# A two-layer graph network: layer 1's factor blocks loaded in two pieces instead of four

## The chip, the cores and the metric

The kernel runs on one core of a Trainium2 chip. The metric is the time of one execution on the device, in microseconds (us). The engines that matter here: TensorE (PE in the profile; its weight loads are PEld) multiplies matrices into eight accumulator banks, VectorE (DVE), ScalarE (ACT) and GpSimd (POOL) work elementwise, and SyncE (SP) issues nearly all transfers between the device's memory and the on-chip memory. Each engine works through its own queue in order; between engines, instructions wait on semaphores.

## The reference

128 samples, each with 128 nodes of 512 features (`x`, 128 x 128 x 512) and a 128 x 128 adjacency (`adj`). Two layers, all in float32:

```python
# layer 0
deg = sum(adj, -1)
agg = (adj @ x) / max(deg, 1e-6)
x = layernorm(x + relu(concat([x, agg], 2) @ W.T))       # W is 512 x 1024
# layer 1
Xw = x @ Wv + bv
e = leaky_relu(sj[:, None, :] + si[:, :, None] + ab[0])   # sj, si = Xw @ halves of aw
t = adj * exp(e);  t = t / (sum(t, -1) + 1e-12)
H = x @ Wk[0] + bk[0] + (t @ x) @ Wk[1] + bk[1] + (t @ t @ x) @ Wk[2] + bk[2]
x = layernorm(x + relu(H))
```

## The kernel before

**Groups and layers.** Four samples make a group, so each layer has 32 groups, numbered 0 to 31 in layer 0 and 32 to 63 in layer 1. Layer 0 runs for all groups, its results go to device memory (`yd`), and layer 1 reads them back.

**The products.** Each large product is done by a fast scheme for 2 x 2 blocks, applied twice: seven outer products (called 1 to 7), each made of seven inner products (k = 1 to 7). An outer product is a task that yields after each inner one: in layer 0 `P12`, `P56`, `P74` do two outer products each, and `T` (function `last`) does product 3 and the multiplication by the normalised adjacency; in layer 1 `O1` to `O7` do one each, and `C` combines. Tables `LEFT` and `RIGHT` say which of the seven sums of a factor the inner product k reads: RIGHT gives 0, 4, 5, 2, 1, 3, 6 in the order in which k is run (1, 5, 6, 2, 7, 3, 4).

**Where the right factors lie.** One tile, `big`, holds them. In layer 0 it is seven slots of 7 x 256 columns (`wf`, table `SLOT`). In layer 1 each outer product o has a block of 7 x 385 columns, `wg[o]`, at the column that `AT` gives. Blocks 1, 2 and 5 lie where the raw weights of layer 1 were staged and which is free long before; blocks 6, 7, 4 and 3 lie one after the other from column 0 on, over the slots of layer 0. So these four can only be loaded as layer 0's last group gives its slots up: slots 0 and 1 are read by `P12`, 2 and 3 by `P56`, 4 and 5 by `P74`, 6 by `T`. The blocks are made earlier, by GpSimd beside layer 0, and are kept in device memory (`wds`, the profile's `wd`). `wg_load(o, i)` brings piece i of block o back. `outer` (L618) asks that all four pieces of its block are issued.

**The order of the work.** It is written out by hand. `PA`, `PT`, `PG`, `PB`, `PL` list the steps of TensorE for a group of layer 0, for the last group of layer 0 with the first of layer 1, and for the groups of layer 1. All else (loads, stores, sums) is placed at a position, two positions to a step, by tables `PLACES_...`. `PLACES_T` (L1038) places the pieces: block 1 at -467, -448, -408 and -388, block 2 at -351, -316, -304 and -263, block 5 at -200, -173, -148 and -104, block 6 at -32, -31, -4 and -2, block 7 at 26, 23, 20 and 65, block 4 at 31, 54, 73 and 46, block 3 at 53, 79, 88 and 85 (pieces 0, 1, 2, 3 each), counted from the start of `PT`. The position decides the order within SyncE's queue, not the time: SyncE runs ahead until an instruction has to wait.

**Around it in SyncE's queue.** `y_store` (L571, issue on L576) stores a half group's result of layer 0 once ScalarE has normalised it (`ln_apply`, L517). `load_y` (L91, issue on L95) loads the input rows of the next half group into one of two buffers, so it waits for the store from that buffer. `residual` (L378, VectorE, L380) adds the product to that y and frees the accumulator bank that the product was in. `load_left` (L86, issue on L83) loads the left factor, `a_load` (L609, also L83) the turned adjacency.

**The steps of one product of layer 1** (`outer`): the first inner product goes to bank X, and ScalarE copies X to bank Y (L628); the second goes to Z and is copied or, with the bias, added by VectorE to `s5` (L632, L634); the third accumulates in X, and VectorE writes W = X + s5 (L637); and so on. In layer 0 `pair` does the same with lines L314, L317, L320 and L326. The banks of `T`, freed by the residuals of group 31, are those that O5 of group 32 takes.

Of the kernel before, what the change touches and what calls it, by code (L numbers as in the profile page):

```python
# [16 lines left out]
def kernel(  # L17
# [219 lines left out]

    def wg_load(o, i):
        assert len(wds) == 7
        k = slice(2 * i, min(2 * i + 2, 7))  # L240
        nc.sync.dma_start(wg[o][:, k], wds[o][:, k])


# [645 lines left out]
    for g in range(1, NG):  # L889
        base[g] = len(steps)  # L890
        for s in PA:
            name, k = s.split(".")
# [8 lines left out]
    for s in PT:  # L901
        name, k = s.split(".")
# [3 lines left out]
    for g in range(NG):  # L906
        base[NG + g] = base[NG] + len(PB) * g
        for s in PL if g == NG - 1 else PB if g else PG:
            name, k = s.split(".")
# [137 lines left out]
    for (name, o, i), pos in PLACES_T.items():  # L1047
        at(max(2 * start_b + pos, 2 * base[NG - 1]) if NG < 20 else 2 * start_b + pos, wg_load, o, i)
# [52 lines left out]
```

## Time and profile before

| | |
|---|---|
| median of 3 runs | 2068.39 us (2068.28 to 2069.03) |
| profiled execution | 2068.23 us, its span 2066.5 us |
| granted TensorE clock | 0.999 |
| TensorE busy | 2053.8 us, 99% of the span |
| VectorE, ScalarE, GpSimd busy | 1515.5, 1161.4, 1374.6 us |
| moved by DMA | 287.14 MB |
| loads of factor blocks (L241) | 21 of 385 KB, 7 of 192.5 KB, from 622.7 to 818.5 us |

The span is the time from the first to the last instruction. A view's line gives the start and the duration in us, the engine, the line of the kernel, the operation, the tiles (written <- read), the shapes, how many alike follow each other, and in brackets the idle time before and what ended it. A DMA's duration on SyncE's queue is that of its issue; its landing comes later. Layer 0 ends and layer 1 begins at about 802 to 820 us.

### The profile page before, as it was taken

Reading aid. Unit: us, or ns where it says so; the run is one execution under the profiler, and the core shown is the slowest. Engines: PE = TensorE matmul, PEld = TensorE weight load, DVE = VectorE, ACT = ScalarE, POOL = GpSimd, SP = SyncE. Lnnn points to the kernel's source line nnn. Section 1 sums busy time; section 2 is a strip of 40 time slices with the busy share of each in tenths; the row PEclk is TensorE's granted clock in tenths of the full one; section 3 lists DMA queues with packets and bytes.
Section 4 is the critical chain, followed back from the end, with each engine's and each line's share of the span. In section 5 each row is a group of like instructions: output and inputs, shape, how many; then the busy total and the mean of one; then the engine's idle time right before and its main releaser. Section 6 shows DMA issues by size and latency. Waiting matters only on the chain.

```text
span 2066.5 us, 25981 instructions
## 1 busy us (share of the span) xinstructions
PE 2053.8 (99%) x7108; PEld 1338.4 (65%) x7108; DVE 1515.5 (73%) x3418; ACT 1161.4 (56%) x2872; POOL 1374.6 (67%) x1263
## 2 busy tenths in 40 slices
PE   9999999999999999999999999999999999999998
PEld 6878888888887887555555555555555555555554
DVE  6787777787878777667767767767766766766766
ACT  2666666666666666455455455455455455455454
POOL 5877888887777776756656656656656656656652
PEclk9999999999999999999999999999999999999999
DMA  9777766666667777434534534534534534534623
GB/s 202 176 192 189 187 188 176 158 190 190 165 162 197 181 189 228 108 88 112 129 88 109 132 88 112 128 88 112 128 88 113 128 88 113 128 87 112 129 75 110
DMA packets 431071, 287.14 MB, mean 139 GB/s; under 512 B 155593, under 2 KB 353865, under 8 KB 430924
## 3 DMA queue, kind: packets, MB, share of 16 engines
q1 hardware_dynamic: 429996, 284.15, 55.6%
q10 hardware_dynamic: 800, 1.31, 0.3%
q8 instruction: 56, 0.92, 0.2%
q14 instruction: 91, 0.75, 0.1%
q0 software_dynamic: 128, 0.01, 0.0%
HBM read 191.60 MB, written 93.79 MB: 138 GB/s over the span
## 4 chain that ended last, share of the span: by engine, by line
PE 98%; DMA 1%; DVE 1%; issue 0%; POOL 0%; ACT 0%; ACTq 0%; SPq 0%; DVEq 0%
PE bA L155 51%; PE bB L155 47%; DMA xb<-in_x_dram 0%; DMA big<-in_w0t_dram 0%; PE bA L181 0%; DVE big L1024 0%; DVE c L458 0%; PE bA L167 0%; DVE c L366 0%; ACT y L562 0%; POOL rs L539 0%; DVE dg L730 0%; DVE bA L475 0%; DVE y L380 0%; DVE xl L259 0%
## 5 line engine op out<-in xcount | busy, mean ns | idle before, releaser
L155 PE MATMUL bB<-big,xu 128*128 128x385 f32 (+1 forms) x1806 | 556.8, 433 | 0.1
L155 PEld LDWEIGHTS bB<-big,xu 128*128 128x128 f32 x1806 | 342.6, 190 | 159.8 <-issue 24.4
L155 PE MATMUL bA<-big,xl 128*128 128x256 f32 (+1 forms) x1358 | 406.0, 416 | 0.6 <-DVE bA L475 0.6
L155 PE MATMUL bB<-big,xs 128*128 128x256 f32 (+1 forms) x1316 | 389.0, 416 | 0.0
L155 PEld LDWEIGHTS bA<-big,xl 128*128 128x128 f32 x1358 | 256.5, 189 | 100.5 <-issue 15.3
L155 PEld LDWEIGHTS bB<-big,xs 128*128 128x128 f32 x1316 | 249.6, 190 | 84.1 <-issue 1.7
L155 PE MATMUL bA<-big,xu 128*128 128x256 f32 (+1 forms) x896 | 287.0, 432 | 0.1
L155 PE MATMUL bA<-c,TT 128*128 128x512 f32 x512 | 240.7, 592 | 0.0
L504 ACT ACTIVATE junk<-y,mv 128x512 bf16<-128x512 f32 x252 | 181.7, 721 | 88.9 <-POOL mv L499 82.6
L499 POOL TENSOR_SCALAR mv<-mv 128x4 f32<-128x4 f32 x63 | 14.4, 228 | 313.0 <-DVE y L380 313.0
L155 PEld LDWEIGHTS bA<-big,xu 128*128 128x128 f32 x896 | 166.5, 189 | 76.6 <-DVE bA L397 5.0
L517 ACT ACTIVATE y<-y,mv,rstd 128x512 f32<-128x512 f32 x252 | 204.7, 814 | 3.6 <-POOL mv L512 1.7
L637 DVE TENSOR_TENSOR bB<-bB,s 128x385 f32<-128x385 f32 x128 | 72.6, 567 | 170.9 <-ACT s L634 73.4
L380 DVE SCALAR_TENSOR_TENSOR y<-bA,y 128x512 f32<-128x512 f32 x253 | 165.7, 681 | 12.0 <-PE bA L155 7.4
L155 PE MATMUL bB<-big,xl 128*128 128x385 f32 (+1 forms) x462 | 172.1, 480 | 0.4 <-ACT bA L456 0.4
L805 POOL TENSOR_TENSOR T<-ag,T 128x512 f32<-128x512 f32 x31 | 39.5, 1274 | 198.7 <-ACT T L800 145.8
L155 PE MATMUL bA<-big,xs 128*128 128x385 f32 x448 | 167.9, 491 | 0.0
L155 PEld LDWEIGHTS bA<-c,TT 128*128 128x128 f32 x512 | 96.8, 189 | 88.8 <-issue 47.6
L270 POOL TENSOR_TENSOR xs<-xl 128x896 f32<-128x896 f32 x63 | 131.4, 2085 | 21.4 <-PE bB L155 21.4
L849 ACT COPY bA<-r 128x512 f32<-128x512 f32 x62 | 36.5, 589 | 190.7 <-DVE big L847 190.6
L282 POOL TENSOR_TENSOR xu<-xu,xs 128x896 f32<-128x896 f32 x63 | 131.5, 2087 | 9.3 <-PE bB L155 9.3
L278 POOL TENSOR_TENSOR xl<-xu,xl 128x896 f32<-128x896 f32 x63 | 133.4, 2117 | 1.1
(206 smaller groups left out, 3614.2 us busy)
## 6 DMA issues: line engine op xcount, KB each, us to landing
xb<-in_x_dram SPq DMA_DIRECT2D x256, 128.0 KB, 3.8
y<-in_x_dram SPq DMA_DIRECT2D x64, 512.0 KB, 4.3
yd<-y SPq DMA_DIRECT2D x64, 512.0 KB, 3.0
xb<-yd SPq DMA_DIRECT2D x256, 128.0 KB, 6.5
y<-yd SPq DMA_DIRECT2D x64, 512.0 KB, 6.8
out_dram<-y SPq DMA_DIRECT2D x62, 512.0 KB, 3.3
ag<-in_adj_dram SPq DMA_DIRECT2D x63, 256.0 KB, 6.0
sb<-sd SPq DMA_DIRECT2D x252, 64.0 KB, 3.3
```

The lines of the kernel that those rows point to most:

```text
L155: nc.tensor.matmul(dst, lhsT, rhs, start=start, stop=True, skip_group_check=True)
L270: S_.tensor_add(xs[n][:, 0], xl[n][:, 0], xl[n][:, 1])
L278: S_.tensor_sub(xl[n][:, 0], xu[n][:, 0], xl[n][:, 0])
L282: S_.tensor_sub(xu[n][:, 1], xu[n][:, 1], xs[n][:, 1])
L380: V.scalar_tensor_tensor(y, t, 0.0, y, ALU.max, ALU.add, accum_out=mvs[n][:, b, 0:1])
L499: S_.tensor_scalar(mvs[n][:, :, 0], mvs[n][:, :, 0], -1.0 / F, None, ALU.mult)
L504: L_.activation(junk, ys[n, b // 2][:, b % 2], AF.Square, bias=mvs[n][:, b, 0:1], accum_out=mvs[n][:, b, 1:2])
L517: L_.activation(y, y, AF.Identity, bias=mvs[n][:, b, 0:1], scale=rstds[n][:, b : b + 1])
L637: V.tensor_add(W, X, s5)
L805: S_.tensor_mul(T, adjs[NG + g], T)
L849: L_.copy(to[b], row(b, 254, 766, 1))
```

## The change

Of the four calls of `wg_load` for a block, the two with odd i do nothing. The call with i = 0 loads inner factors 0 to 3 (770 KB), the one with i = 2 factors 4 to 6 (577.5 KB). The positions stay, so factors 2 and 3 are loaded at the place of piece 0 and factor 6 at the place of piece 2.

```diff
     def wg_load(o, i):
         assert len(wds) == 7
-        k = slice(2 * i, min(2 * i + 2, 7))
+        if i % 2:
+            return
+        k = slice(2 * i, min(2 * i + 4, 7))
         nc.sync.dma_start(wg[o][:, k], wds[o][:, k])
```

## The prediction

> **What bounds the kernel now.** I read the page first: the busy shares and the chain that ended last.
>
> ```profile
> PE 2053.8 (99%) x7108; PEld 1338.4 (65%) x7108; DVE 1515.5 (73%) x3418; ACT 1161.4 (56%) x2872; POOL 1374.6 (67%) x1263
> ...
> PE 98%; DMA 1%; DVE 1%; issue 0%; POOL 0%; ACT 0%; ACTq 0%; SPq 0%; DVEq 0%
> ```
>
> TensorE is busy all the way and the chain is 98% TensorE. Then the list of waits, for TensorE alone:
>
> ```profile
> PE bA L152 <- POOL ident masks.py:199: 2.7, 1, 2.7
> PE bA L155 <- DVE bA L475: 0.6, 2, 0.3
> PE bB L155 <- ACT bA L456: 0.4, 1, 0.4
> ```
>
> These are all the waits of TensorE that the list has: 3.7 us, all at the very start, and none is for a load of a factor block. So there is hardly anything to win: the change can move the time only by opening a hole in TensorE's row. The question is which transfer comes later, and whether anybody on TensorE's path is waiting for it.
>
> Third, the timeline of SyncE's queue where layer 0 ends and layer 1 begins:
>
> ```profile
> 785.85 0.34 SPq L241 DMA_DIRECT2D big<-wd  x1
> 786.87 0.36 SPq L576 DMA_DIRECT2D yd<-y  x1
> 787.33 0.42 SPq L241 DMA_DIRECT2D big<-wd  x1
> 787.84 3.47 SPq L95 DMA_DIRECT2D y<-in_x_dram  x2
> ...
> 802.55 1.34 SPq L241 DMA_DIRECT2D big<-wd  x3
> 808.13 0.37 SPq L576 DMA_DIRECT2D yd<-y  x1
> 808.60 0.41 SPq L241 DMA_DIRECT2D big<-wd  x1
> 809.54 0.37 SPq L576 DMA_DIRECT2D yd<-y  x1
> 811.30 3.53 SPq L95 DMA_DIRECT2D y<-in_x_dram  x2
> 814.92 4.31 SPq L241 DMA_DIRECT2D big<-wd  x8
> ```
>
> By the positions in PLACES_T, 785.85 and 787.33 are pieces 0 and 1 of block 6; the three at 802.55 are pieces 2, 1, 0 of block 7; 808.60 is piece 0 of block 4; the eight at 814.92 are the rest of blocks 7, 4 and 3. Between them stand stores of y of group 30 (L576) and loads of y of group 31 (L95), which go into the buffers that those stores empty: a load of y cannot be issued before the store has landed.
>
> Last, VectorE, ScalarE and TensorE where that y is used (start, duration, engine, line, operation, tiles, shapes, count, idle time before):
>
> ```profile
> 815.82 0.69 DVE L380 SCALAR_TENSOR_TENSOR y<-bA,y 128x512 f32<-128x512 f32 x1 [0.57 <-PE bA L155]
> ...
> 820.14 0.65 DVE L380 SCALAR_TENSOR_TENSOR y<-bA,y 128x512 f32<-128x512 f32 x1
> ...
> 822.88 0.56 DVE L637 TENSOR_TENSOR bA<-bA,s 128x385 f32<-128x385 f32 x1
> ...
> 820.90 0.46 ACT L628 COPY bA<-bA 128x385 f32<-128x385 f32 x1 [3.86 <-DVE y L380]
> ...
> 821.83 1.46 PE L155 MATMUL bA<-big,xs 128*128 128x385 f32 x4
> ...
> 823.77 0.81 PE L155 MATMUL bA<-big,xs 128*128 128x385 f32 x2
> ```
>
> The load of y issued at 811.30 takes 4.4 us to land (the tile's own view), so it lands at 815.74; the matmul that the residual at 815.82 also needs had ended at 815.54. This residual starts 0.08 after the landing: it is already waiting for y, not for TensorE. From there VectorE runs without a gap until 823.44.
>
> **The change, part by part.** Bytes first: before 21 loads of 385 KB and 7 of 192.5 KB, after 7 of 770 and 7 of 577.5, both 9,432.5 KB. 14 issues go. At a median of 431 ns each that is 6.0 us of SyncE, worth nothing: SyncE is waiting for ScalarE or VectorE both before and after each of these places (after the eight at 814.92 its next instruction is at 828.61, held by ScalarE). If that cover were gone the gain would be at most the 1.0 us of TensorE's other start-up waits, which no such load causes: 0.
>
> *Blocks 1, 2, 5 (622 to 754 us).* They go to memory that was free long before, and are first read at 803.8 or later. Pieces 0 and 1 of block 1 were issued back to back already. Piece 1 of block 2, now at 662.30, stands ahead of the load of y at 662.85 that lands 5.35 later, at 668.20, with its residual at 670.09: 1.9 us in hand against the 0.98 us worked out below. Block 5's stands ahead of four loads (sb) that are used more than ten microseconds later; block 1's last, half as large, ahead of one load of y. Cost 0; at the slower rate below, 2.06, at worst 0.2.
>
> *Block 6.* SyncE's own list of waits shows that these loads wait for layer 0's products:
>
> ```profile
> SPq L241 <- PE bB L155: 3.7, 4, 2.7
> ```
>
> The longest, 2.7 us, ends at 785.85, when the product that reads factor 3 of slot 0 is done. The new piece also covers factor 6, which the next product reads: SyncE waits four matmuls longer, which the chain has at 0.86 us, and the store of y at 786.87 stands behind 770 KB. The loads of y of group 30 (787.84 and 790.94) come 0.4 to 0.9 us later, and so do their residuals at 793.62 and 795.93, which end on a landing of y already. Behind them in VectorE's queue the first operation that TensorE needs soon is L326, 798.80 to 799.50, for a matmul at 800.32. Idle gaps of 0.40 and 0.17 us in the queue swallow part, the 0.8 ahead of the matmul the rest. Cost 0; if the second y came 1.3 late and no gap helped, 0.5.
>
> *Block 7.* Piece 3 comes forward from position 65 to 20: 192.5 KB more at 802.55. The region was last read by P56, whose last matmul ends at 801.35, so no new wait. The first of the three loads lands 3.7 after its issue, at 806.2, the others 0.98 each behind it, 808.2; 0.5 more, or 0.9 with what block 6 hands on, is 809.1. The store issued at 808.13 begins to move at 809 only (the DMA share of 808 to 809 is 0.00). Cost 0, at worst 0.2.
>
> *Block 4, the one that costs.* At 808.60 the load becomes 770 KB. The store of y at 809.54 stands behind it, and behind that the load of y issued at 811.30. For the rate I take the stretch in which nothing but such loads moves (us, busy times by engine, clock, DMA share, GB/s):
>
> ```profile
> 805.00:807.00 2.00, 2.00 (x8) 1.43 (x8) 1.04 (x3) 1.54 (x4) 1.92 (x2) 1.00 1.02 404
> ...
> 810.00:812.00 2.00, 2.00 (x8) 1.08 (x6) 1.03 (x4) 1.20 (x3) 2.00 (x2) 1.00 0.92 191
> ```
>
> 385 KB (394,240 bytes) at 404 GB/s are 0.98 us. From 812 to 815 the DMA engines are fully busy with these transfers in turn, so the lateness goes through: y lands at 816.72 and the residual moves from 815.82 to 816.80. The second row, the stretch in which this very load starts, would give 2.06 us; it is nearest in place, but I read its slow part as the start of a transfer, which a longer one pays once, so I take 0.98 and keep 2.06 as the upper end. Lower end 0, if transfers of one queue do not hold each other up; a gain is excluded, since nothing ahead of this y becomes smaller.
>
> What it does to TensorE: VectorE has no gap, so all behind it moves by 0.98. ScalarE's copy at 820.90, into the bank that the third residual frees, goes to 821.88 to 822.34. The matmul at 821.83 (third product of O5) overwrites the copy's source and must wait. Where the trace shows such a pair, the copy that ends at 805.08 and the matmul after it at 805.23, 0.15 lies between. So 822.49 instead of 821.83: 0.66. Then VectorE's L637 ends at 824.42 instead of 823.44, and the matmul that waits for it, due at 823.77 + 0.66, starts at 824.57: 0.80 in all. VectorE's next idle 1.19 us (before 824.62) ends the chain. With 2.06 the same steps give 825.65 against 823.77: 1.9.
>
> *Blocks 4 and 3, the rest.* After the last load of y come three transfers of 1,925 KB in all instead of eight of 2,502.5 KB; they land earlier than the 825.5 of before. O4's first two products run from 832.2, O3's from 838.6: 7 us in hand. Cost 0.
>
> Sum: the profiled execution took 2068.23 us (span 2066.5 and 1.7 around it), 0.16 under the median of the runs, 2068.39. Adding 0.80 to the median gives **2069.2 us**. Ends: 0, and 1.9 + 0.5 + 0.2 + 0.2 = 2.8.
>
> **Two rules of the Trainium skill.** The eight loads at 814.92 are issued over 3.6 us and the last lands 6.9 us after its issue, at 825.5: their waiting times overlap. "DMA: Bandwidth & Descriptors", section "Anatomy of one DMA", gives each transfer (fitted on GpSimd's path) about 2.0 us of fixed cost besides its bytes; 14 fewer would by that be an estimated 28 us gained if they ran one by one. By the row above they don't, and nobody waits for them: 0. Against the change speaks "Perfetto Trace Analysis", section "DMA Optimizations": pieces may let some work start sooner. That would matter for the blocks' own first products; with 7 us in hand the sum by it is the same 0.
>
> **The rivals.** All within or beyond 0.2%, which is 4.1 us and about what a measurement of this kernel can tell from no change.
> 1. *Hidden after all:* the rings share their time, the y is late by under 0.2 us, no hole. For it: ScalarE's copy ends 0.47 us before the matmul that needs it, so the first 0.3 us of lateness cost nothing. Against: the load of y at 811.30, with two transfers ahead of it, took 4.4 us, the next one, with less ahead, 3.6. Time 2068.4, with 0.3 either way.
> 2. *A larger hole, 1.5 to 4.1 us:* the slow rate of 191 GB/s and the late store of block 6 add up: 1.9 + 0.5. Time about 2070.8. Against: the 0.8 us that the matmul at 800.32 has in hand.
> 3. *Slower by over 0.2%:* the load of y at 811.30 comes so late that VectorE's queue holds TensorE for more than 4.1 us. It decides from a lateness of 4.1 + 0.2 = 4.3 us, that is 394,240 bytes at 92 GB/s. No stretch with such packets is that slow here. Time from 2072.6.
> 4. *Faster by over 0.2%:* would need 4.1 us back, and TensorE waits for 3.7 in all, at the start.
>
> **How the numbers follow.** Chances: forecast (a hole of 0.3 to 1.5) 0.55, rival 1 0.27, rival 2 0.10, rival 3 0.06, rival 4 0.02. Within 0.2% are the first three, 0.92; slower 0.06; faster 0.02. Rival 1's lower edge is 2068.1; the forecast's own range is 2068.7 to 2069.9. The range 2068.0 to 2070.5 takes in both, and the near part of rival 2.
>
> **What the profile after would show.** The 14 loads; the load of block 4 at about 808.6 with a landing near 5.5 us instead of 4.5; the load of y after it landing about 1 us later; the residual of 815.82 near 816.8; a new row of TensorE's waits for ScalarE L628 or VectorE L637, under 1 us, near 822 to 825. If TensorE has no new gap there and the time stays, rival 1 was right. I am wrong if TensorE stands still elsewhere: at 800 (block 6), at 832 or 838 (a block that came too late), or in layer 0.

## The result, and the profile after

| | before | after |
|---|---|---|
| median (range), 19 runs each | 2068.2 us (2067.93 to 2069.03) | 2071.49 us (2070.32 to 2073.3) |
| span of the profiled execution | 2066.5 us | 2069.3 us |

The ratio is 1.0016, with a 95% interval of 1.001 to 1.0023. The kernel lost 3.3 us; 2069.2 was forecast, and the range ended at 2070.5. The loss is less than the 0.2% that the prediction drew as its bound, but it is a loss.

The page of the kernel after, its busy times and the shares of the chain that ended last:

```profile
PE 2053.9 (99%) x7108; PEld 1339.7 (65%) x7108; DVE 1515.3 (73%) x3418; ACT 1160.9 (56%) x2872; POOL 1374.8 (66%) x1263
...
PE 97%; DMA 1%; DVE 1%; issue 0%; ACT 0%; POOL 0%; ACTq 0%; SPq 0%; DVEq 0%
```

No engine works longer: TensorE has 0.1 us more than before. So the 2.8 us of span are time in which TensorE stood still. Its list of waits, after (engine, tile, line, what it waited for: us in total, times, longest):

```profile
PE bA L152 <- POOL ident masks.py:199: 2.7, 1, 2.7
PE bA L155 <- DVE y L382: 1.6, 2, 1.1
PE bA L155 <- DVE big L1018: 0.7, 1, 0.7
PE bA L155 <- ACT bA L630: 0.7, 1, 0.7
PE bA L155 <- DVE bA L477: 0.6, 2, 0.3
PE bB L155 <- ACT bA L458: 0.4, 1, 0.4
```

(Lines of the kernel from L241 on count two more after the change: the residual L380 is now L382, ScalarE's copy L628 is L630, the load of a block L241 is L243.) New are the two waits for the residual, L382, and the one for the copy, L630. The 0.7 for L1018 lies at the start of the program, where the profiles of the other kernels below have 0.3 to 0.5 or nothing; since no matmul up to 791 starts later than before, it has nothing to do with the loss. The timeline of TensorE, after, has the three holes (start, duration, tiles, shapes, count, and in brackets the idle time before and its end):

```profile
795.77 1.13 PE L155 MATMUL bA<-big,xl 128*128 128x256 f32 x4 [0.50 <-DVE y L382]
...
822.52 0.91 PE L155 MATMUL bA<-big,xs 128*128 128x385 f32 x2 [1.08 <-DVE y L382]
823.27 0.81 PE L155 MATMUL bB<-big,xu 128*128 128x385 f32 x2
824.75 1.56 PE L155 MATMUL bA<-big,xs 128*128 128x385 f32 x4 [0.67 <-ACT bA L630]
```

The brackets count from the modelled end of the matmul before. What a hole really costs is read better from the starts of the same matmuls in the two timelines:

| matmul of before | before | after | after minus before |
|---|---|---|---|
| T's multiplication by the adjacency | 791.70 | 791.67 | -0.03 |
| second product of outer 4, layer 0 | 796.01 | 796.74 | 0.73 |
| first product of O5 | 819.90 | 820.63 | 0.73 |
| the product after the hole at 822.52 | 821.19 | 823.27 | 2.08 |
| third product of O5 | 821.83 | 824.75 | 2.92 |
| 3 us later | 825.07 | 828.22 | 3.15 |

So nothing is lost before 791; 0.76 at 795.77, 1.35 at 822.52, 0.84 at 824.75 and 0.2 more behind it: 3.2 us in all. The spans of the two profiled executions differ by 2.8, the medians by 3.3. From 828 to 860 the difference does not grow, so nothing is lost at 832 or 838: no factor block came too late.

What made those residuals late is in SyncE's queue, after:

```profile
786.68 0.34 SPq L243 DMA_DIRECT2D big<-wd  x1
787.12 0.39 SPq L578 DMA_DIRECT2D yd<-y  x1
787.60 5.88 SPq L95 DMA_DIRECT2D y<-in_x_dram  x2
793.57 0.42 SPq L588 DMA_DIRECT2D sd<-an  x1
...
798.32 3.07 SPq L83 DMA_DIRECT2D sb<-sd  x4
801.49 4.58 SPq L83 DMA_DIRECT2D xb<-yd  x4
806.17 0.87 SPq L243 DMA_DIRECT2D big<-wd  x2
808.86 0.37 SPq L578 DMA_DIRECT2D yd<-y  x1
809.33 0.41 SPq L243 DMA_DIRECT2D big<-wd  x1
810.27 0.82 SPq L578 DMA_DIRECT2D yd<-y  x1
814.18 4.02 SPq L95 DMA_DIRECT2D y<-in_x_dram  x2
```

Read beside the rows of before, this gives the chain. (When the store of y at 787 landed is not in the trace; it is taken from the load that waits for it and that is issued right behind.)

| | before | after |
|---|---|---|
| block 6's first load issued | 785.85 | 786.68 |
| the store of y behind it issued, landed | 786.87, 790.92 | 787.12, 793.09 |
| the load of y into the emptied buffer issued | 790.94 | 793.10 |
| residuals of group 30 that wait for y | 793.62 and 795.93 | 795.02 and 797.48 |
| the store sd<-an issued; the loads of sb, which wait for its landing | 792.14; 796.55 | 793.57; 798.32 |
| the first load of xb behind them issued, and how long its issue took | 799.49, 1.49 | 801.49, 3.09 |
| block 7's first load issued | 802.55 | 806.17 |
| the store of y issued, its landing after | 808.13, 3.1 | 808.86, 5.2 |
| the load of y of group 31 issued, landed | 811.30, 815.74 | 814.18, 819.08 |
| the residual of O5's bank | 815.82 | 819.15 |
| ScalarE's copy behind it | 820.90 | 824.24 |

Block 6's load was issued 0.83 later, and was twice as large. The store behind it was issued only 0.25 later but landed 2.17 later, and the next load of y can't be issued until it has landed. While SyncE waited for that, the DMA engines ran out of work. Windows of both kernels, first before (us, then busy times of TensorE, its weight loads, VectorE, ScalarE, GpSimd, then the clock, the DMA share and GB/s):

```profile
786.00:789.00 3.00, 3.00 (x16) 2.60 (x15) 2.56 (x9) 2.22 (x7) 2.38 (x2) 1.00 0.71 212
793.00:796.00 3.00, 3.00 (x10) 1.69 (x9) 1.98 (x6) 0.00 (x0) 0.72 (x1) 1.00 1.01 309
801.00:805.00 4.00, 4.00 (x18) 3.01 (x16) 3.74 (x10) 1.94 (x5) 2.97 (x5) 1.00 0.88 195
```

and after:

```profile
786.00:789.00 3.00, 3.00 (x16) 2.60 (x15) 2.60 (x9) 2.18 (x7) 2.36 (x2) 1.00 0.46 68
793.00:796.00 3.00, 2.50 (x7) 0.94 (x6) 0.98 (x3) 0.00 (x0) 0.72 (x1) 1.00 0.62 196
801.00:805.00 4.00, 4.00 (x20) 3.43 (x19) 3.87 (x10) 2.24 (x6) 3.65 (x7) 1.00 1.02 147
```

Where the engines were full, at a share of 1.01, they are at 0.62. That work was not saved but pushed on, and the lateness grew from 0.83 to 3.62 us: the two landings that SyncE waits for brought 2.0 of it (the loads of sb and xb), and the single issue of 3.09 us at 801.49 the other 1.6. In that stretch the DMA engines were full (1.02). Whether they held the issue up or a wait for VectorE, to which the list of SyncE's waits puts 3.1 us there, is open. Block 7's loads left at 806.17, ahead of the store of y at 808.86, which itself was issued only 0.73 later. The Trainium skill, "DMA: Bandwidth & Descriptors", section "Two DMAs through the same engine are not ordered", says that within one queue of one DMA engine the descriptors start in order. The row of the store at 787.12 agrees: with 770 KB ahead of it, where there were 385, it landed 5.97 us after its issue instead of 4.05.

The timeline of VectorE, after, shows the three late residuals (in brackets, what ended the idle time):

```profile
795.02 0.69 DVE L382 SCALAR_TENSOR_TENSOR y<-bA,y 128x512 f32<-128x512 f32 x1 [2.72 <-DMA y<-in_x_dram]
...
797.48 0.69 DVE L382 SCALAR_TENSOR_TENSOR y<-bA,y 128x512 f32<-128x512 f32 x1 [0.54 <-DMA y<-in_x_dram]
...
819.15 0.69 DVE L382 SCALAR_TENSOR_TENSOR y<-bA,y 128x512 f32<-128x512 f32 x1 [3.17 <-PE bB L155]
```

The first frees at 795.71 the bank that outer 4's first product takes at 795.77. In the kernel before it ended at 794.31 and the product started at 795.15: 0.84 in hand, used up. The third bracket names a product of TensorE, but that is not the releaser: its y landed at 819.08, 0.07 before the residual. The engine named had long been done.

### The profile page after: what moved, and what is told of

Read it like the earlier page. It is cut to its first block, busy times and chain, and to the rows that moved or that the text cites. A ratio compares the mean times of both kernels' runs of the same rounds, so it can differ in the third digit from the quotient of the medians.

```text
span 2069.3 us, 25959 instructions
## 1 busy us (share of the span) xinstructions
PE 2053.9 (99%) x7108; PEld 1339.7 (65%) x7108; DVE 1515.3 (73%) x3418; ACT 1160.9 (56%) x2872; POOL 1374.8 (66%) x1263
## 4 chain that ended last, share of the span: by engine, by line
PE 97%; DMA 1%; DVE 1%; issue 0%; ACT 0%; POOL 0%; ACTq 0%; SPq 0%; DVEq 0%
PE bA L155 50%; PE bB L155 47%; DMA xb<-in_x_dram 0%; DMA y<-in_x_dram 0%; DMA big<-in_w0t_dram 0%; PE bA L181 0%; DVE y L382 0%; ACT junk L599 0%; DVE big L1026 0%; DVE c L460 0%; PE bA L167 0%; DVE c L671 0%; DVE c L368 0%; ACT y L564 0%; POOL rs L541 0%
## 5 line engine op out<-in xcount | busy, mean ns | idle before, releaser
L382 DVE SCALAR_TENSOR_TENSOR y<-bA,y 128x512 f32<-128x512 f32 x253 | 165.7, 681 | 16.0 <-PE bA L155 5.2
```

The costliest lines, as they stand in the source:

```text
L382: V.scalar_tensor_tensor(y, t, 0.0, y, ALU.max, ALU.add, accum_out=mvs[n][:, b, 0:1])
```

## The experiments

**Theories.** A: each enlarged load holds up the store and the load of y behind it in SyncE's queue. It begins at block 6; the delay is handed on through the gate "a load of y is issued when the store has landed" to block 7's and block 4's place, and TensorE stands where the late y's banks are needed. B, the rival: the blocks act one by one, without handing on, and block 6 costs little. A further question was whether it is the bytes or the longer rows (6,160 bytes for each of 128 partitions and load, where there were 3,080), and for block 6, whether the bytes or the wait for one more product.

The kernel before was run beside them and had medians of 2068.2 to 2068.6, so differences below 0.3 us are not read. The ratios' intervals are about 0.1% to either side, 2 us. By them alone only the change, block 6 alone and "block 6 later" have intervals clear of 1. For the others the reading rests on the medians of ten runs together with the holes in the profile. A profile shows one of the ten, and not always a typical one: those of the exchange of pieces below and of block 7 alone are of a short execution, those of blocks 1, 2 and 5 and of all blocks as short loads of a long one. Holes are counted from the starts of the same matmuls, from T's multiplication by the adjacency on (791.70 in the kernel before).

### One part alone

Each is the kernel before, with this in place of the one line, for the blocks in the brackets:

```diff
-        k = slice(2 * i, min(2 * i + 2, 7))
+        if o in (6,):              # (1, 2, 5) / (7,) / (4,) / (1, 2, 5, 7, 4, 3)
+            if i % 2:
+                return
+            k = slice(2 * i, min(2 * i + 4, 7))
+        else:
+            k = slice(2 * i, min(2 * i + 2, 7))
```

**Blocks 1, 2 and 5 alone.**

> Blocks 1, 2 and 5 in two pieces, the other four blocks in four as before. Both theories: nothing waits for these loads and what is queued behind them has slack, so no hole in TensorE's row and the time of before, 2068.2 us (0.2 either way). If over 0.5 us of the 3.3 us show here, a third cause lies in layer 0.

Measured 2068.30 (2068.06 to 2068.96) beside 2068.34: 0.0. By the median the early loads cost nothing and gain nothing. Its profile, of an execution of 2068.92, does have a hole, against the expectation: 0.55 at 796.

```profile
PE bA L155 <- DVE y L385: 0.3, 1, 0.3
```

Nothing near 796 was changed here; the first load of y took 6.9 us to land there instead of 5.7. So a hole of half a us at this place also comes without a larger load, and one such hole in a profile proves little. Those of the change and of block 6 alone are 0.8 to 0.9.

**Block 6 alone.**

> Block 6 alone in two pieces. Theory A (one delay that is handed on): the load waits for one more product, moves twice the bytes ahead of a store of y, and from there all of SyncE's queue runs late: a hole of about 0.8 us at 796, the loads of block 7 issued about 3 us later than 802.55, the residual of 815.82 late by about 2 us and a second hole of 1 us or more at 822; time 2069.8 to 2071.2. Theory B (each block costs by itself, where it stands): only the hole at 796, 0.8 us; time 2069.0.

Measured 2070.29 (2069.57 to 2070.87): +1.95, ratio interval 1.0001 to 1.0019. This is more than half of the whole loss, from a block that the prediction gave 0. Its queue of SyncE:

```profile
786.45 0.34 SPq L246 DMA_DIRECT2D big<-wd  x1
786.88 0.39 SPq L581 DMA_DIRECT2D yd<-y  x1
787.36 5.96 SPq L95 DMA_DIRECT2D y<-in_x_dram  x2
...
806.15 1.34 SPq L246 DMA_DIRECT2D big<-wd  x3
...
813.52 2.60 SPq L95 DMA_DIRECT2D y<-in_x_dram  x2
```

The three loads of block 7 are those of the kernel before, unchanged, and still leave at 806.15 instead of 802.55 (802.3 to 803.4 in all profiles with block 6 in four pieces at its old places); the load of y of group 31 leaves at 813.52 instead of 811.30. TensorE waits at both places, though only the first was touched:

```profile
PE bA L155 <- DVE y L385: 1.0, 2, 0.6
PE bA L155 <- ACT bA L633: 0.7, 1, 0.7
```

The delay is handed on. B has no room for this.

**Block 7 alone.**

> Block 7 alone in two pieces (its last 192.5 KB come forward). Theory A: its loads land at about 808.6 instead of 808.1, before the store of y behind them moves; no hole, 2068.2 us. Theory B: the store lands about 0.5 us later, and of that nothing to 0.3 us reaches TensorE; at most 2068.6.

Measured 2069.16 (2068.24 to 2070.07): +0.82. Both theories had less. In its profile the residual moves to 816.19 and the matmuls' starts show a hole of 0.46 there and one of 0.2 at 796. That even 192.5 KB more ahead of the store are felt is likely; with an interval of the ratio of 0.9994 to 1.0013 it is not shown by this run alone.

**Block 4 alone.**

> Block 4 alone in two pieces. Theory A: the load of y behind it lands 1.0 us late (by the full rate) to 1.8 us late (if the first packets of rows twice as long take twice as long, as the load of block 6 showed after the change), hole of 0.6 to 1.7 us near 822; time 2068.8 to 2069.9. Theory B: the whole second part of the loss, 2.3 us, is block 4's; time 2070.5.

Measured 2069.68 (2069.52 to 2071.09): +1.34. The load of y leaves at 811.30, as before, but lands 5.8 us later instead of 4.4; the residual is about 1.6 late (T's multiplication starts 0.28 earlier in this profile), and by the starts of the matmuls there are two holes, 0.37 and 0.84, at the second and the third product of O5, and 0.24 behind them. This is the mechanism of the prediction; the size is not. The windows where the load runs, first of this kernel, then of the kernel before, then of the change:

```profile
810.00:814.00 4.00, 4.00 (x16) 2.75 (x15) 2.36 (x5) 2.44 (x5) 1.80 (x1) 1.00 0.94 236
810.00:814.00 4.00, 4.00 (x16) 2.71 (x15) 2.65 (x6) 2.69 (x6) 2.07 (x2) 1.00 0.98 296
810.00:814.00 4.00, 4.00 (x17) 2.73 (x16) 2.49 (x7) 3.00 (x8) 2.87 (x2) 1.00 1.03 390
```

All that moved in this stretch moved at 236 GB/s. At that rate 394,240 bytes take 1.67 us, not the 0.98 that 404 GB/s gave. The load itself landed after 6.2 us, against 4.5 before: 1.7 more. But the slow rate does not belong to the place: in the change, where block 7's late loads were still moving until this load's turn came, the same stretch ran at 390.

**All but block 6.**

> All blocks in two pieces except block 6, which keeps its four. By theory A block 6 starts the lateness that the others add to: no hole at 796, block 7's loads issued near 802.5 again, and what stays is what blocks 7 and 4 cost by themselves, 0.8 and 1.3 in their own runs: 2069.5 to 2070.5. If the blocks simply add (B), the change minus block 6's own 1.95: 2069.5. If block 6 did not matter beside the others: 2071.5.

Measured 2069.63 (2069.25 to 2071.05) beside 2068.55: +1.08. The hole at 796 is gone, block 7's loads leave at 802.89:

```profile
802.89 0.87 SPq L246 DMA_DIRECT2D big<-wd  x2
...
811.34 5.12 SPq L95 DMA_DIRECT2D y<-in_x_dram  x2
```

So without block 6 nothing is handed on, and what is left is about block 4's own loss. The time itself does not choose between the theories: A's range and B's 2069.5 lie too near each other. The single losses, 1.95 + 0.82 + 1.34 = 4.1, are more than the 3.3 of the change; that they fall on the same y, so that its lateness is paid once, is likely but not shown.

### What in block 6 costs: the wait or the bytes

**The wait alone.** In the kernel before, pieces 0 and 1 change places. Piece 1, which needs the later product, now stands ahead of the store; no load is larger.

```diff
-("wg_load", 6, 1): -31 ... ("wg_load", 6, 0): -32
+("wg_load", 6, 1): -32 ... ("wg_load", 6, 0): -31
```

> The kernel before, with pieces 0 and 1 of block 6 exchanged: the first of them now waits one product longer (0.86 us), with the same 385 KB ahead of the store of y. It shows the wait by itself. If the wait carries the loss of block 6 (1.95 in its own run), 2069.5 or more; if the bytes do, at most a hole of 0.3 at 796 and 2068.2 to 2068.8.

Measured 2069.44 (2068.53 to 2070.72) beside 2068.55: +0.89. The first load leaves at 786.49. The median is just below what was given for the wait and well above what was given for the bytes. The profile, of 2068.53, the shortest of the ten, has a hole of 0.37 at 795, no more than chance gave above.

**All the bytes, with the first half ahead of the wait.** Block 6 alone at two places, but each place issues two short loads, the first of which need not wait:

```diff
-        k = slice(2 * i, min(2 * i + 2, 7))
-        nc.sync.dma_start(wg[o][:, k], wds[o][:, k])
+        if o == 6 and i % 2:
+            return
+        for j in (2 * i, 2 * i + 2) if o == 6 else (2 * i,):
+            k = slice(j, min(j + 2, 7))
+            nc.sync.dma_start(wg[o][:, k], wds[o][:, k])
```

> Block 6 alone, all at the two places of the change, but each load as two with rows of 3,080 bytes (the last of 1,540). Against block 6 in two loads (1.95 us over before) and the exchange of its pieces (0.9 over before): the bytes ahead of y are those of the former, the packets those of the latter; the first piece goes out 0.86 earlier than the merged load. If long packets carry the difference, 0.2 to 1.0 us over before; if the bytes do, 1.5 to 2.

Measured 2069.07 (2067.68 to 2069.84) beside 2068.28: +0.79. This lies in the range that was given for the packets, not in the one for the bytes. The wait is in this run too: the second short load needs the later product, and the store behind it leaves at 787.27, counted from T's multiplication as late as in block 6 alone. So 0.89 and 0.79 are not two parts of one sum. The traces part them better than the medians, by the second load of y, which is issued when that store has landed. In the kernel before, with the pieces exchanged, as short loads, and as one load:

```profile
790.94 0.38 SPq L95 DMA_DIRECT2D y<-in_x_dram  x1
791.60 0.38 SPq L95 DMA_DIRECT2D y<-in_x_dram  x1
792.17 0.37 SPq L95 DMA_DIRECT2D y<-in_x_dram  x1
792.95 0.37 SPq L95 DMA_DIRECT2D y<-in_x_dram  x1
```

| | before | exchanged | short loads | one load |
|---|---|---|---|---|
| start of T's multiplication | 791.70 | 791.48 | 791.83 | 791.43 |
| second load of y, counted from it | -0.76 | 0.12 | 0.34 | 1.52 |
| later than before | | 0.88 | 1.10 | 2.28 |

In the other profiles with block 6 in its four pieces the load is at -0.8 to -0.5, so steps of 0.3 say little here. The wait alone makes the load of y 0.9 late. All the bytes ahead of the store, as short loads, add about 0.2, no more than the scatter. The other 1.2 come when they are one load: then the first half waits too, and the rows are twice as long. No run parts these two.

### Bytes or longer rows

**All blocks, at the two places, as short loads:** the loop of the last edit without the condition on o.

> All blocks: the same factors at the same two places as after the change, but each load issued as two (385 + 385 and 385 + 192.5 KB), so that a row's packet is 3,080 bytes again and not 6,160. If the loss is only the bytes that stand ahead of the stores and loads of y and the longer wait (theory Q), the time is that of the change, 2071.5 us. If the first packets of long rows, 1105 ns against 562 ns, are part of it (theory P), each merged load ahead of a y costs 0.5 to 0.8 less, and the time is 2069 to 2070.5.

Measured 2070.41 (2069.77 to 2071.5) beside 2068.55: +1.86. This lies in theory P's range. In its profile there is no hole at 796, while those at 820 to 825 stay; they come to 3.6 us, more than in the change, in an execution of 2071.48, the second longest of the ten. So what making one load of two adds, the longer rows and block 6's first half held back, explains at most the 1.4 us between the medians of this and the change.

**Block 4 alone, as short loads.**

> Block 4 alone, at the two places of the change, each load as two with rows of 3,080 bytes. No wait for a product plays a part here. If the bytes alone set the lateness, the time of block 4 in two loads, 1.3 us over before (1.0 to 1.6). If long packets make their start slower, half of it or less, 0.2 to 0.8 over before. With 0.98 us of lateness, as the prediction had it, 0.8.

Measured 2069.87 (2069.43 to 2070.83) beside 2068.28: +1.59, where the one long load cost 1.34. At this place the rows' length is not the cause; what the two runs share is the bytes at that place. Its window:

```profile
810.00:814.00 4.00, 4.00 (x16) 2.75 (x15) 2.70 (x6) 2.75 (x6) 2.14 (x2) 1.00 0.98 261
```

261 GB/s with short rows and 236 with long ones: both far below the 404 that the prediction took, and below the 390 of the change.

### The place

If the place in the queue is what costs, the same large loads must be free behind the loads of y. All five are the change, with other positions in `PLACES_T`.

**Block 6's first load behind the loads of y of group 30.**

```diff
-("wg_load", 6, 0): -32
+("wg_load", 6, 0): -24
```

> The change, with block 6's first load placed behind the two loads of y instead of ahead of them (position -24 instead of -32); nothing else. It is first read 30 us later, so it cannot be late itself. Theory A: y of group 30 lands as before or earlier, no hole at 796; block 7's loads as early as before to 1 us later; the time of the run without block 6, 2069.5 to 2070.5. If not the place ahead of y but the size of the load matters, 2071.5.

Measured 2071.18 (2070.41 to 2074.24) beside 2068.55: +2.63, more than A gave. The hole at 796 is gone, but its queue of SyncE shows that the load had only moved the crush along:

```profile
795.00 2.43 SPq L243 DMA_DIRECT2D big<-wd  x2
...
804.26 0.87 SPq L243 DMA_DIRECT2D big<-wd  x2
...
812.45 5.54 SPq L95 DMA_DIRECT2D y<-in_x_dram  x2
```

Block 7's loads leave at 804.26, between the 802.55 of before and the 806.17 of the change, and y of group 31 lands at 818.87, 0.21 sooner than in the change. A was incomplete: the place at 786 is one, block 7's and block 4's places around the store at 808 are others, and sparing the first alone is not enough.

**Block 4's first load behind the loads of y of group 31.**

```diff
-("wg_load", 4, 0): 31
+("wg_load", 4, 0): 45
```

> The change, with block 4's first load behind the two loads of y of group 31 (position 45 instead of 31). If that load, standing ahead of y, makes the second hole (1.3 us by itself, 2.3 in the change), the holes near 822 shrink to under 1 us and the hole of 0.8 at 796 stays: 2069.3 to 2070. If the second hole comes from the lateness that block 6 hands on through block 7's loads, it stays above 1.5 us and the time at 2070.5 to 2071.5.

Measured 2069.03 (2068.49 to 2070.62) beside 2068.24: +0.79, a little below its first range. Only the hole at 796 is left; at 822 there is none, though block 7's loads still leave late (805.15). Here that lateness makes no hole at 822, where TensorE itself comes 0.9 later; in the next run, where it does not, it makes one.

**Both of these.**

> The change, with the first loads of blocks 6 and 4 both behind the loads of y next to them. No hole at 796. If places ahead of y are all there is, only block 7's two loads can still hold up the store of y at 808: holes of 0 to 0.8 us, 2068.3 to 2069.3. If not, 2070 or more.

Measured 2068.88 (2068.31 to 2069.47): +0.64, with one hole of 0.6 at 822. It is gone when block 7's loads are moved too (the last run below), so it is theirs.

**Blocks 7 and 4 behind the loads of y, block 6 at its place.**

```diff
-("wg_load", 7, 0): 26 ... ("wg_load", 7, 2): 20 ... ("wg_load", 4, 0): 31
+("wg_load", 7, 0): 44 ... ("wg_load", 7, 2): 44 ... ("wg_load", 4, 0): 45
```

> The change, with blocks 7 and 4 behind the loads of y of group 31, block 6 where it was. The hole at 796 alone, 0.8 us, and none at 822 if the lateness that block 6 hands on is only harmful together with loads ahead of y: 2068.9 to 2069.5.

Measured 2068.72 (2068.66 to 2069.02): +0.48, below its range, with the one hole at 796, 0.84.

**All three behind the loads of y:** the last edit, and block 6 at -24.

> The change, with blocks 6, 7 and 4 all behind the loads of y next to them (positions -24, 44, 44, 45). Nothing merged stands ahead of a y any more: y of both groups lands as before or earlier, no hole at 796 or 822, 2068.0 to 2068.5, the time of before with 14 transfers fewer. If the large loads cost by themselves wherever they stand, 2069 or more.

Measured **2067.91 (2067.81 to 2068.02)** beside 2068.24: -0.33, just below its range. Its queue of SyncE, and all waits of TensorE:

```profile
807.86 1.79 SPq L578 DMA_DIRECT2D yd<-y  x2
810.74 1.88 SPq L95 DMA_DIRECT2D y<-in_x_dram  x2
812.72 3.46 SPq L243 DMA_DIRECT2D big<-wd  x6
```

```profile
PE bA L152 <- POOL ident masks.py:199: 2.7, 1, 2.7
PE bB L155 <- ACT bA L458: 0.4, 1, 0.4
PE bA L155 <- DVE bA L477: 0.3, 1, 0.3
```

No residual and no copy is waited for any more. The stores land in 2.9 to 3.0 us and the load of y in 3.6. All bytes of the change are moved, in the change's transfers: the place alone, and with it what a load waits for and what waits behind it, decides between 2071.49 and 2067.91. All ten runs lie below all 31 of the kernel before, but the interval of the ratio (0.9989 to 1.0007) holds 1; that the version is as fast as the kernel before is shown, that it is faster is likely. Where its 0.3 us comes from is open.

## Why the prediction was right or wrong

**What bounds the kernel: right.** TensorE is the bound, the change could only open holes, and the whole loss is holes of TensorE. That 14 issues fewer are worth nothing also held: blocks 1, 2 and 5 alone moved the time by 0.0. One reading under it was too broad: SyncE does not wait for ScalarE or VectorE at each of these places. At block 6's it waits for TensorE, and before the load of y for the landing of a store, and on these two waits the loss turned. The estimate of 28 us, from the fixed cost that the Trainium skill gives in "DMA: Bandwidth & Descriptors", section "Anatomy of one DMA", did not come: with the places mended, the gain was at most 0.3 us. That fits transfers whose waiting times overlap, as the prediction said.

**Blocks 1, 2 and 5, cost 0: right.** **Blocks 4 and 3, the rest, cost 0: right**, there is no hole at 832 or 838.

**Block 6, cost 0, at worst 0.5: this step failed.** It cost 1.95 alone. The issue was forecast right (0.86 later; measured 0.83), and the wait for the extra product counts. Three readings went wrong behind it. First, the step had the residuals 0.4 to 0.9 late; they came 1.40 and 1.55 late. It counted the wait, which by itself makes the load of y 0.9 late, and put the larger load ahead of the store at nothing; as one load it made y's load 2.2 to 2.3 late in all. Second, it looked for the next consumer in VectorE's own queue (L326, for the matmul at 800.32) and overlooked the bank that the residual itself frees: outer 4's first product had 0.84 in hand, and 0.76 was lost there. Even this 0.84 is of one execution; in that of blocks 1, 2 and 5 alone it was used up without block 6's help. Third, it let the delay end at VectorE's next idle time, while in SyncE's queue it went on.

**Block 7, cost 0, at worst 0.2: failed with it.** The working had its loads "with what block 6 hands on" 0.4 later, near 803. They left at 806.17, 3.6 later, and so were still ahead of the store of y at 808.86, which landed after 5.2 us instead of 3.1. Alone the step was worth 0.82 by the medians, with an interval of the ratio that holds 1.

**Block 4, 0.98 us late and 0.80 of holes: the mechanism was right, the size was not.** The store of y, the load, the residual, the copy, O5's product: all stood in the profile after in that order. Alone, the load made y about 1.6 late, not 0.98, and the time 1.34 longer. The mis-sized term for block 4 alone is the rate: 404 GB/s, from the place where loads follow each other, instead of the 191 of the stretch in which this very load starts. Measured were 236. The prediction noted that the 191 was nearest in place, and explained it away as a start that is paid once. In the change itself the stretch ran at 390 and the residual was still 3.33 late: 2.88 of it was there when the load of y was issued, with the late landing of the store in front of it, and 0.46 came between issue and landing (4.9 us instead of 4.4). A second wait, for the residual itself at 822.52, stood in front of the one foreseen at 824.75.

**The sum** was +0.80, its upper end 2.8; +3.3 came. Rival 2, a larger hole because the slow rate of block 4 and the late store of block 6 add up, comes nearest to what happened, though in the change the rate was not slow. It had a chance of 0.10 because of "the 0.8 us that the matmul at 800.32 has in hand", which belonged to another consumer. Its 2070.8 still was 0.7 too low: it added the two, and between them the delay grew. That a hole elsewhere would prove the prediction wrong was said; it came at 796.

**Open:** why block 4's load runs at 236 to 261 GB/s at 810 to 814 when it alone is enlarged, while the same stretch ran at 390 in the change and the loads of block 7 at 404 at 805 to 807. For block 4 the rows' length is not it. Open too is whether block 6's 1.2 us are its longer rows or its first half held back, and why one issue took 3.09 us at 801.49.

## What to carry to other kernels

A transfer that nobody waits for still has a price if a store, whose landing a later load waits for, stands behind it in the same queue: put bulk loads behind such pairs. Do not size such a load by the rate of a stretch where loads follow each other: here 404 GB/s stood against 236 in one kernel, and 390 in another at the same place. When a step is made later, list every consumer of what it frees (here the bank of the residual), not only the next instruction in its engine's queue. And follow a delay through the whole in-order queue: with a landing gate in it, 0.8 us at 786 were 3.6 us at 806.

## What was not expected of the hardware

- A load issued 0.83 us later led, 20 us on, to loads issued 3.62 us later in the same queue. Between them the DMA engines stood partly idle (a share of 0.62 for 3 us, 1.01 before), because SyncE had waited until 793.10 for a store to land while more work stood behind in its queue.
- 385 KB more ahead of a store in one long load made it land 1.9 us later after its issue (5.97 instead of 4.05), about twice what the rate of back-to-back loads, 404 GB/s, gives. As two short loads, the first of which left earlier, the same bytes made it 0.8 (4.89).
- One load of 770 KB took 6.2 us to land where 385 KB took 4.5, with the stretch at 236 GB/s; with the engines busy ahead of it the same stretch ran at 390.
- Saving 14 of 28 transfers brought at most 0.3 us.
